# Turning the attention context on VectorE instead of TensorE, in a list-scheduled conditioned transformer block

## The chip, the cores and the metric

The kernel runs on one core of one Trainium2 chip. The metric is device time in microseconds (us), the median of several runs. Five engines work side by side and meet at semaphores: TensorE (PE; its weight loads are listed as PEld), VectorE (DVE), ScalarE (ACT), GpSimd (POOL) and SyncE (SP), which issues nearly all DMAs here. Matmul results land in PSUM, which has eight banks of 128 partitions x 512 fp32 numbers.

## The reference: what is computed

Eight sequences of 512 tokens and 256 channels go through four layers; all is fp32.

```
emb = silu(sin_emb(timestep)) @ W_ada + b_ada          # scale and shift for the norm
x   = layernorm(src) * (1 + scale) + shift
q, k, v = x @ Wq + bq, ...                             # 16 heads of 16 channels
scores = q k^T / 4 + attention_bias; masked keys = -inf
ctx = softmax(scores) @ v                              # per head, heads put side by side again
x   = x + (ctx @ Wo + bo)
x   = x + gelu2(layernorm(x) * g2 + beta2 ...) @ W2 + b2
x   = adapter(x); x = rotation(x); x = adapter(x)      # adapters of width 64, chosen by domain
```

The attention bias is 8 x 16 x 512 x 512 numbers, 134 MB, read once.

## The kernel before, in words

**Tiling.** The work of a batch is cut into 16 *units*: a head group g of four heads, and a tile qt of 128 queries. There are 128 units; n numbers them. A *half* is two query tiles; both tiles of a half in one head group are a *pair* of units. Order: batch, half, head group, tile.

**A unit** (`attention`). Four DMAs load the bias, 256 KB each, into four of 16 `bias` buffers (L898). POOL adds the mask to each (L902). PE forms four score matrices at once in four strips of its array (L910). DVE takes the bias minus the scores and its row minimum `low` (L922); ACT takes the exponential (L926), in place. Then the probabilities must be turned so that keys lie on partitions. Two ways do this. In a *turned* group, two of the four heads are transposed in 32x32 blocks by DVE (L937, `tb`) and four DMAs put the blocks in place (L946, `pT`). The other heads are transposed by PE against the identity (L961) and copied out of PSUM by ACT or DVE (`evict`, L682). `turned_groups` says which groups are turned: only group 3 in the first batch, groups 0 to 2 in the last, all in between.

**A pair.** After its second unit, PE multiplies probabilities and values (L987): `pv`, 128 x 256 in PSUM, holds four heads in four strips of 32 partitions (16 channels, then the softmax sum in row 16), with queries along the free axis. It is then brought to the layout "queries on partitions" in four steps: ACT or DVE copies pv to `pvs` (L682), PE transposes it back in two pieces (`back`, L1005), DVE takes the reciprocal of the sums (L1014) and multiplies by it (L1015) from PSUM into `ctx`.

**A half's finish** (`finish`). `half_transposed` turns ctx again by four PE transposes (L724) and copies the result out to `hT` (L682), because the output projection (L748) needs channels on partitions. Residual, layer norm, feed-forward (L1043, L1068; a gelu through ACT, POOL and DVE, L1052, L1055, L1059), two adapters with norms and the rotation, and the store (L1179) follow. The last half is finished tile by tile.

**Who sets the order.** Each step is a `Task` of a `Plan` with an engine (or a choice of ACT and DVE), a cost, what it reads and writes, and a rank. `Plan.run` plays the list through once while the kernel is built: each engine takes the ready task of the lowest rank for which buffers are free; the resulting order is then emitted as it stands, engine by engine. So costs and ranks decide the order of each engine's instructions, and who copies what out of PSUM. In that list a DMA occupies SP for its cost, and its data pass one common queue:

```
if e == DMA:
    queues = max(queues, now) + t.data
    seen = max(seen, queues)
seen += self.AFTER[e]
```

In the built program each DMA that SP issues also carries a wait for the landing of the DMA eight places before it.

The finish of half n is spread over ranks n+2 to n+11, or to n+19 for the last ones (`n < 110`). `late_weights` holds the loads of wv, bv, wo, w1, w2 (1 MB each), wd and rows2, each with a rank; `experts_matrices` fetches 16 small expert matrices by addresses that SP reads (L1210, L1214).

Of the kernel before, what the change touches and what calls it, by code (L numbers as in the profile page):

```python
# [16 lines left out]
ALU = mybir.AluOpType  # L17
AX = mybir.AxisListType

P = 128  # L20
# [49 lines left out]


class Task:
    def __init__(self, costs, emit, rank, mode, at, data):
        self.costs, self.emit, self.rank, self.data = costs, emit, rank, data
        self.engine = None
        self.mode, self.at = mode, at
        self.waits, self.then, self.buffers = 0, [], []


class Plan:  # L80

    AFTER = {PE: 0.22, DVE: 0.14, ACT: 0.16, POOL: 0.12, DMA: 2.4}

    def __init__(self):
        self.tasks, self.written, self.read = [], {}, {}
        self.rank, self.stream = 0.0, None

    def __call__(self, engine, cost, emit, r=(), w=(), mode=None, at=0.0, data=0.0):  # L90


        if isinstance(engine, dict):
            task = Task(engine, emit, self.rank, mode, at, data)
        else:
            task = Task({engine: cost}, lambda e: emit(), self.rank, mode, at, data)
        needs = []
        for key in r:
            if key in self.written:
                needs.append(self.written[key])  # L100
        for key in w:
            if key in self.written:
                needs.append(self.written[key])
            needs.extend(self.read.pop(key, ()))
        for key in r:
            self.read.setdefault(key, []).append(task)
        for key in w:
            self.written[key] = task
        for other in {id(o): o for o in needs if o is not task}.values():
            other.then.append(task)  # L110
            task.waits += 1
        for key in (*r, *w):
            buffer = key[0] if isinstance(key, tuple) else key
            if isinstance(buffer, Buffer) and buffer not in task.buffers:
                task.buffers.append(buffer)
                buffer.left += 1
        self.tasks.append(task)
        if self.stream is not None:
            self.stream.append(task)
        return task  # L120
# [23 lines left out]
    def run(self, free_at):  # L144
# [9 lines left out]
            heapq.heappush(events, (at, seq, "free", e))  # L154
            seq += 1
        idle = set()
        now, queues = 0.0, 0.0
        while events:
            now, _, what, x = heapq.heappop(events)
            if what == "ready":  # L160
# [13 lines left out]
            for e in [e for e in free_at if e in idle]:  # L174
# [29 lines left out]
                if t.mode is not None and t.mode != mode[e]:  # L204
                    cost += 1.3 if e == ACT else 0.1
                    mode[e] = t.mode
                idle.discard(e)
                t.start, t.end = now, now + cost
                order.append(t)
                heapq.heappush(events, (t.end, seq, "free", e))  # L210
                seen = t.end
                if e == DMA:
                    queues = max(queues, now) + t.data
                    seen = max(seen, queues)
                seen += self.AFTER[e]
                heapq.heappush(events, (seen, seq + 1, "over", t))
                seq += 2
# [12 lines left out]
def conditioned_sequence_kernel(  # L230
# [37 lines left out]
    SC = Slots(banks[:4])  # L268
    BG = Slots(banks[4:], SC)
    RES = slots("res", 3, [P, NT, D])  # L270
    M8 = slots("m8", 2, [P, NT, S], mybir.dt.uint8)
    NEG = slots("neg", 5, [P, S], BF16)
    MOD = slots("mod", 1, [P, 2, D])
    ROT = slots("rot", 1, [P, 2, D])
# [7 lines left out]
    PT = slots("pT", 2, [P, 4 * NT * 2 * P])  # L282
    TB = slots("tb", 2, [P, TURNED * S])
    PVS = slots("pvs", 2, [P, 2 * P])
    INV = slots("inv", 2, [P, 2, 4])
    CTX = slots("ctx", 2, [P, 2, H, HD])
    HT = slots("hT", 2, [P, NC, 2 * P])
    TMP = slots("tmp", 2, [P, 2, D])
    GT = slots("gT", 1, [P, NF, 2 * P])
# [70 lines left out]

    def turned_groups(b):

        return 3 if b == 0 else 0, NG - 1 if b == B - 1 else NG

    def rows_of(t, r, n):
        return t[:, r : r + 1, :].to_broadcast([P, n, D])
# [182 lines left out]
            b1s, cols[:, C_B1 : C_B1 + NF], AF.Copy, scale=0.851), [], ["b1s"], at=4.0)  # L549

    def late_weights():
        wo_rows = w_o.rearrange("(c m e) n -> m e c n", c=NC, e=32)

        def load(rank, cost, data, emit, key):
            plan.rank = rank
            plan(DMA, cost, emit, [], [key], data=data)

        load(-1.5, 0.45, 0.8, lambda: nc.sync.dma_start(
            wv, w_v.rearrange("(c p) n -> p c n", p=P)), "wv")
        load(-1.4, 0.4, 0.4, lambda: nc.sync.dma_start(  # L560
            bv_row, rows_in[R_BV * D : (R_BV + 1) * D].partition_broadcast(P)), "bv")
        load(2.5, 1.0, 1.0, lambda: [
            nc.sync.dma_start(wo[:, c], wo_rows[:, :HD, c]) for c in range(NC)
        ], "wo")
        load(1.1, 0.45, 3.0, lambda: nc.sync.dma_start(
            w1, w_1.rearrange("(c p) n -> p c n", p=P)), "w1")
        load(1.2, 0.45, 3.0, lambda: nc.sync.dma_start(
            w2, w_2.rearrange("(c p) n -> p c n", p=P)), "w2")
        load(2.6, 0.5, 0.5, lambda: nc.sync.dma_start(
            wd, down_w.rearrange("l (c p) a -> p l c a", p=P)), "wd")  # L570
        load(1.3, 0.4, 0.8, lambda: nc.sync.dma_start(
            rows2, rows_in[(R_GAM + 1) * D : (R_BET + 2) * D].rearrange(
                "(r d) -> r d", d=D)[::2].partition_broadcast(P)), "rows2")

    def rotations():
# [14 lines left out]
                )  # L590
            nc.sync.dma_start(cc.t[B : B + 1], rows_in[None, R_B2 * D : (R_B2 + 1) * D])

        plan(DMA, 1.0, load, [], [gb, (cc, "b2")], data=0.2)
        plan.rank = 2.5
        four = "p (g u v) -> p g u v"

# [26 lines left out]
        def store():  # L623
# [1 line left out]
            nc.sync.dma_start(turned_rows, cc.t[:B])  # L625

        plan(DMA, 0.7, store, [*((ab, u, v) for u in range(2) for v in (None, 0, 1)), (cc, "c")],
             ["rot_rows", "turned_rows"], data=0.2)

        def bias_rows():  # L630

# [7 lines left out]
            nc.sync.dma_start(wu[A1:K1, 1], turned_rows)  # L639

        plan.rank = 6.8
        plan(DMA, 1.6, bias_rows, ["turned_rows"], ["wu"], data=0.6)
        plan.rank = 7.0
        ps = Buffer(BG, lambda t: t[:, : NC * (B + 1)].rearrange("p (c b) -> p c b", c=NC))

# [112 lines left out]
    def prepare(b):  # L758
# [96 lines left out]
            for m in range(4):  # L855
                nc.sync.dma_start(to[m, :, :size], v_pad.t[32 * m : 32 * m + 32, :size])

        plan(DMA, 1.8, turned_values, [(v_pad, t) for t in range(NT)], [v_turn], data=1.0)
        negs = [Buffer(NEG) for _ in range(NT)]
        for t in range(NT):  # L860
            plan(ACT, 0.52, lambda t=t: nc.scalar.activation(
# [26 lines left out]
    def attention(u, n):  # L888
# [60 lines left out]

        if turned:  # L950
            plan(DMA, 2.5, moved, [(tb, j) for j in range(turned)], [(pT, i)],
                 data=1.05 * TURNED)
        plan.rank = n + 0.0

        whole = "p (j k i q c) -> p j k i q c"
# [22 lines left out]
        def values():  # L978
            for kc in range(NT):
# [14 lines left out]
             [(v_pad, t) for t in range(NT)] + ([v_turn] if turned else [])  # L994
             + [(pT, a, j) for a in range(2) for j in range(turned, 4)]
             + [(pT, a) for a in range(2) if turned], [pv], mode="col")
        sb = Buffer(PVS)
        evict(lambda: (
            sb.t.rearrange("p (q i c) -> p i q c", i=4, q=2),
            pv.t.rearrange("p (i q c) -> p i q c", i=4, q=2)), [pv], [sb], 0.255, 0.34)  # L1000
        pc = Buffer(BG, lambda t: t[:, : 2 * P].rearrange("p (i j e) -> p i j e", i=2, j=4))

        def back():
            for a in range(2):
                nc.tensor.transpose(  # L1005
                    pc.t[:, a].rearrange("p j e -> p (j e)"), sb.t[:, a * P : (a + 1) * P],
                    ident,
                )

        plan(PE, 0.22, back, [sb], [pc], mode="full")  # L1010
        inv = Buffer(INV)

        def normalise():
            nc.vector.reciprocal(inv.t, pc.t[:, :, :, HD])  # L1014
            nc.vector.tensor_tensor(  # L1015
                ctx_h.t[:, :, 4 * g : 4 * g + 4, :], pc.t[:, :, :, :HD],
                inv.t.unsqueeze(3).to_broadcast([P, 2, 4, HD]), ALU.mult,
            )

        plan(DVE, 0.45, normalise, [pc], [inv, (ctx_h, g)])  # L1020


    def feed_forward(res, rk, ts, store=None):
# [132 lines left out]
    def finish(b, ts, store=None):  # L1156
        res, keys = state[b][0], state[b][1]
        rk = [keys[t] for t in ts]
        rows = slice(ts[0], ts[0] + len(ts))
        ctx_h = live[(b, ts[0] // 2)]  # L1160
        cT, ck = half_transposed(
            lambda t: ctx_h.t[:, t % 2].rearrange("p h d -> p (h d)"),
            [(ctx_h, g) for g in range(NG)], ts,
        )
        token_tiles(
            len(ts),
            lambda i: [(cT.t[:, c, i * P : (i + 1) * P], wo[:, c, :]) for c in range(NC)],
            [*ck, "wo"],
            lambda ps: nc.vector.tensor_tensor(res.t[:, rows], ps, res.t[:, rows], ALU.add), rk,
        )  # L1170
        if ts[0] == 0:
            rots[b] = rot = Buffer(ROT)
            plan(DMA, 0.4, lambda: nc.sync.dma_start(
                rot.t.rearrange("p r d -> p (r d)"), rot_rows[b].partition_broadcast(P)),
                ["rot_rows"], [rot], data=0.9)
        feed_forward(res, rk, ts, store)
        adapter(b, 0, res, rk, ts)
        adapter(b, 1, res, rk, ts)
        plan(DMA, 0.42, lambda: nc.sync.dma_start(  # L1179
            out[b].rearrange("(t p) d -> p t d", p=P)[:, rows], res.t[:, rows]), rk, [],  # L1180
            data=0.4 * len(ts))
# [4 lines left out]
    def experts_matrices():  # L1186
# [19 lines left out]
        for b in range(B):  # L1206
# [10 lines left out]
                            "o p a -> (o p) a"),  # L1217
                    )

            plan(DMA, 2.0, fetch, ["expert"], [(raw, b)], data=0.2)  # L1220

        def kept():
            nc.gpsimd.tensor_tensor(
# [43 lines left out]
    for n, u in enumerate(units):  # L1267
# [5 lines left out]
        if n % 8 == 7:  # L1273
            half = n // 8 % 2
            if n + 1 < len(units):
                plan.begin()
                finish(u[0], [2 * half, 2 * half + 1])
                plan.end(n + 2.0, n + (11.0 if n < 110 else 19.0))
                continue

            for t in range(2):
                plan.begin()
                finish(u[0], [2 + t], Buffer(PT, lambda p: p.rearrange(
                    "p (c q) -> p c q", q=2 * P)[:, :NF]) if t else None)
                plan.end(n + 2.0 + 4 * t, n + 11.0 + 4 * t)
# [97 lines left out]
```

## Time and profile before

| what | value |
|---|---|
| median of 3 runs | 932.08 us (930.09 to 932.15) |
| the profiled execution's own time | 929.78 us |
| its span | 927.8 us |
| mean granted PE clock in it | 0.988 |
| DMA | 216.48 MB, 233 GB/s on average |
| bias loads / pT<-tb transfers | 512 of 256 KB / 448 of 128 KB |

How to read the profile: an engine's busy time is the time in which it has an instruction under way; matmuls overlap, so their busy times are longer than the room that they take. A group such as "L1015 DVE TENSOR_TENSOR ctx<-bank,inv" is all instructions of one line, engine and shape, as output<-inputs; after the bar stand its busy us, the mean ns of one, and the idle time of the engine just before them with what ended it. The chain of waits goes back from the last instruction, at each step to whatever released it.

### The profile page before, as it was taken

To read this page: it belongs to the slowest core of one execution; us is meant where nothing else is said; L and a number is where in the kernel's file an instruction comes from. 1 tells how busy PE (TensorE), PEld (TensorE's weight loads), DVE (VectorE), ACT (ScalarE), POOL (GpSimd) and SP (SyncE) were. 2 spreads that over 40 slices of the span, in tenths; PEclk is the share of its full clock that TensorE was granted. 3 is DMA by queue.
4 is the path that set the end of the run, shared out by engine and by line. 5 is a ranking of instruction groups with operands and counts; after the bars stand their busy time and mean duration, and the time that the engine had idled before them with its cause. 6 is when DMAs were issued, how large, how long until landed. Compare 5 with 4: busy or idle time off the path is not lost.

```text
span 927.8 us, 21009 instructions
## 1 busy us (share of the span) xinstructions
PE 893.6 (96%) x6654; PEld 591.8 (64%) x6654; DVE 788.3 (85%) x2152; ACT 752.7 (81%) x1387; POOL 754.0 (81%) x843
## 2 busy tenths in 40 slices
PE   9989999999999999999999999999999999899994
PEld 7545766566666666667666666666666676566783
DVE  4557888988988989889998889989899899999666
ACT  5957869969898889969799697987989697998553
POOL 7589899987998878978798887989789788989132
PEclk9989999999999999999999999999999999999997
DMA  9578487787977879796966979877895978978000
GB/s 318 192 240 280 151 285 230 215 285 208 300 231 233 262 235 301 203 292 216 315 216 215 303 223 281 261 247 243 251 289 164 288 229 275 288 235 270 18 24 24
DMA packets 160913, 216.48 MB, mean 233 GB/s; under 512 B 18911, under 2 KB 91657, under 8 KB 160802
## 3 DMA queue, kind: packets, MB, share of 16 engines
q1 hardware_dynamic: 160758, 215.12, 73.7%
q8 instruction: 53, 0.87, 0.4%
q14 instruction: 58, 0.48, 0.2%
q10 hardware_dynamic: 44, 0.02, 0.0%
HBM read 149.89 MB, written 4.24 MB: 166 GB/s over the span
## 4 chain that ended last, share of the span: by engine, by line
PE 59%; ACT 10%; DMA 10%; DVE 9%; POOL 6%; issue 4%; SPq 2%; POOLq 0%; DVEq 0%; ACTq 0%
PE bank L910 10%; PE bank L1068 9%; PE bank L961 9%; PE bank L1043 9%; PE bank L987 8%; PE bank L748 4%; DMA bias<-in_bias 4%; PE bank L800 4%; POOL bias L902 3%; ACT bias L926 3%; DMA pT<-tb 2%; DVE bias L922 2%; PE bank L724 2%; ACT pT L682 2%; PE bank L838 1%
## 5 line engine op out<-in xcount | busy, mean ns | idle before, releaser
L902 POOL TENSOR_TENSOR bias<-bias,neg 128x512 f32<-128x512 f32 x512 | 580.1, 1161 | 81.6 <-DMA bias<-in_bias 63.7
L926 ACT ACTIVATE bias<-bias,low 128x512 f32<-128x512 f32 x512 | 344.8, 722 | 62.0 <-DVE low L922 61.2
L922 DVE CUSTOM_DVE_ANT_0 bias<-bank,bias 128x512 f32<-128x512 f32 x512 | 329.7, 684 | 48.3 <-PE bank L910 35.2
L961 PEld LDWEIGHTS bank<-shifted,bias 128*128 128x128 f32 x1152 | 129.0, 142 | 57.1 <-issue 21.6
L961 PE MATMUL bank<-shifted,bias 128*128 128x128 f32 x1152 | 159.3, 279 | 4.5 <-ACT pT L682 2.3
L937 DVE STREAM_TRANSPOSE tb<-bias 128x512 f32<-128x512 f32 x224 | 148.0, 691 | 11.1 <-DMA pT<-tb 8.6
L910 PE MATMUL bank<-kT,qz 32*128 32x512 f32 x1024 | 155.2, 645 | 2.0 <-DVE low L922 1.9
L682 ACT COPY pT<-bank 128x512 f32<-128x512 f32 x209 | 114.3, 588 | 36.1 <-PE bank L961 34.5
L1043 PE MATMUL bank<-hT,w 128*128 128x256 f32 (+1 forms) x544 | 127.1, 374 | 2.1 <-ACT pT L682 0.8
L987 PE MATMUL bank<-pT,v_pad 128*32 128x256 f32 x1152 | 123.0, 382 | 0.0
L1068 PE MATMUL bank<-w,gT 128*128 128x256 f32 x496 | 117.8, 384 | 0.1
L987 PE MATMUL bank<-pT,v_turn 128*32 128x256 f32 x896 | 107.6, 382 | 2.0 <-DMA pT<-tb 2.0
L1043 PEld LDWEIGHTS bank<-hT,w 128*128 128x128 f32 x544 | 94.2, 190 | 23.9 <-issue 4.0
L1068 PEld LDWEIGHTS bank<-w,gT 128*128 128x128 f32 x496 | 90.4, 190 | 26.8 <-issue 13.5
L987 PEld LDWEIGHTS bank<-pT,v_turn 128*32 128x32 f32 x896 | 48.0, 109 | 49.7 <-issue 5.3
L910 PEld LDWEIGHTS bank<-kT,qz 32*128 32x128 f32 x1024 | 44.0, 184 | 46.6 <-issue 26.8
L1055 POOL TENSOR_SCALAR sig<-sig 128x512 f32<-128x512 f32 (+1 forms) x68 | 40.5, 596 | 40.1 <-ACT sig L1052 35.0
L1052 ACT ACTIVATE sig<-bank,b1s 128x256 f32<-128x256 f32 (+1 forms) x136 | 55.0, 456 | 9.9 <-PE bank L1043 9.4
L1059 DVE SCALAR_TENSOR_TENSOR gT<-bank,cols,sig 128x256 f32<-128x256 f32 (+1 forms) x128 | 53.5, 464 | 10.5 <-POOL sig L1055 10.4
L987 PEld LDWEIGHTS bank<-pT,v_pad 128*32 128x32 f32 x1152 | 54.8, 109 | 7.9 <-issue 1.9
L690 DVE BATCH_NORM_STATS2 st<-res 128x6 f32<-128x256 f32 x128 | 52.3, 409 | 5.4 <-DMA res<-in_x 3.5
L682 DVE COPY pT<-bank 128x512 f32<-128x512 f32 x79 | 52.5, 682 | 3.8 <-PE bank L961 3.4
(142 smaller groups left out, 1156.3 us busy)
## 6 DMA issues: line engine op xcount, KB each, us to landing
bias<-in_bias SPq DMA_DIRECT2D x512, 256.0 KB
pT<-tb SPq DMA_DIRECT2D x448, 128.0 KB
out<-res SPq DMA_DIRECT2D x15, 256.0 KB
res<-in_x SPq DMA_DIRECT2D x7, 512.0 KB
v_turn<-v_pad SPq DMA_DIRECT2D x32, 68.0 KB
m<-in_mask SPq DMA_DIRECT2D x8, 256.0 KB
w<-in_w SPq DMA_DIRECT2D x2, 1024.0 KB
mod<-ada_rows SPq DMA_DIRECT2D x8, 256.0 KB
```

The lines of the kernel that those rows point to most:

```text
L682: nc.scalar.copy(*pair()) if e == ACT else nc.vector.tensor_copy(*pair())), r, w)
L902: plan(POOL, 1.12, lambda j=j: nc.gpsimd.tensor_tensor(dif[j].t, dif[j].t, negs[qt].t, ALU.add), [negs[qt]], [dif[j]])
L910: nc.tensor.matmul(sc[j].t, qz.t[strip, par, c, qs], kT.t[strip, c, :], start=True, stop=True,)
L922: plan(DVE, 0.61, lambda j=j: nc.vector.tensor_tensor_reduce(dif[j].t, sc[j].t, dif[j].t, -1.0, 3.0e38, ALU.add, ALU.min, low.t[:, j : j + ...
L926: plan(ACT, 0.61, lambda j=j: nc.scalar.activation(dif[j].t, dif[j].t, AF.Exp, bias=low.t[:, j : j + 1], scale=-1.0), [(low, j)], [dif[j]] ...
L937: plan(DVE, 0.62, lambda j=j: nc.vector.transpose(tb.t.rearrange("p (m h k c) -> h p k m c", m=4, h=TURNED, k=NT)[j], dif[j].t.rearrange(" ...
L961: nc.tensor.transpose(ps.t[:, kc, :], dif[j].t[:, kc * P : (kc + 1) * P], ident)
L987: nc.tensor.matmul(pv.t[32 * j : 32 * j + 32, :], (v_turn if j < turned else v_pad).t[:, at : at + 32], pj, start=(kc == 0), stop=(kc == N ...
L1043: nc.tensor.matmul(ps.t[:, i, :w], w1[:, c, f * P : (f + 1) * P], hT.t[:, c, :w], start=(c == 0), stop=(c == NC - 1),)
L1052: plan(ACT, 0.155 + 0.1 * n, lambda i=i, f=f, ps=ps, sg=sg: nc.scalar.activation(sg.t[:, i, :w], ps.t[:, i, :w], AF.Tanh, bias=b1s[:, f : ...
L1059: plan(DVE, 0.14 + 0.13 * n, lambda i=i, f=f, ps=ps, sg=sg: nc.vector.scalar_tensor_tensor(gT.t[:, f, :w], ps.t[:, i, :w], cols[:, C_B1 + ...
L1068: nc.tensor.matmul(ps.t[:, i, :], gT.t[:, f, i * P : (i + 1) * P], w2[:, f, :], start=(f == 0), stop=(f == NF - 1),)
```

## The change

The context no longer passes PE on its way from the values to the output projection. DVE transposes pv in 32x32 blocks straight out of PSUM into `pvs`, so that queries lie on partitions within each block; reciprocal and multiplication work on that in SBUF and write `zed`, which holds two head groups side by side (32 channels per block); every second head group, DVE transposes zed in blocks into `ctx`, now laid out with channels on partitions. Within a strip of 32 partitions the channels stand in another order than before, so the rows of wo are loaded to match, by eight DMAs instead of two. `finish` uses ctx as it is.

The list changes too: a DMA task may consist of `many` transfers, each of which starts only when the one eight places before it has landed, and the common queue starts with a backlog of 9 us. Ranks of the weight loads change (wo 2.5 to 3.0, w1 1.1 to 3.1, w2 1.2 to 4.1). There is one mask buffer instead of two. In the last batch all four groups are turned. The longer spread of the finish starts at n = 100 instead of 110.

```diff
+    BACKLOG = 9.0
+    FLIGHT = 8
...
+                if e == DMA:
+                    begun = now
+                    for _ in range(t.many):
+                        begun = max(begun, landed[-self.FLIGHT]) + cost / t.many
+                        queues = max(queues, begun) + t.data / t.many
+                        landed.append(queues + 1.5)
+                    cost = begun - now
...
                 if e == DMA:
-                    queues = max(queues, now) + t.data
-                    seen = max(seen, queues)
+                    seen = max(seen, queues - 0.4)
...
-    M8 = slots("m8", 2, [P, NT, S], mybir.dt.uint8)
+    M8 = slots("m8", 1, [P, NT, S], mybir.dt.uint8)
...
-        return 3 if b == 0 else 0, NG - 1 if b == B - 1 else NG
+        return (NG - 1 if b == 0 else 0), NG
...
-        load(2.5, 1.0, 1.0, lambda: [
-            nc.sync.dma_start(wo[:, c], wo_rows[:, :HD, c]) for c in range(NC)
-        ], "wo")
-        load(1.1, 0.45, 3.0, lambda: nc.sync.dma_start(
+        load(3.0, 3.6, 1.0, lambda: [
+            nc.sync.dma_start(wo[32 * j : 32 * j + 32, c], wo_rows[c, j, :, :HD])
+            for c in range(NC) for j in range(4)
+        ], "wo", many=8)
+        load(3.1, 0.45, 3.0, lambda: nc.sync.dma_start(
             w1, w_1.rearrange("(c p) n -> p c n", p=P)), "w1")
-        load(1.2, 0.45, 3.0, lambda: nc.sync.dma_start(
+        load(4.1, 0.45, 3.0, lambda: nc.sync.dma_start(
             w2, w_2.rearrange("(c p) n -> p c n", p=P)), "w2")
...
-        sb = Buffer(PVS)
-        evict(lambda: (
-            sb.t.rearrange("p (q i c) -> p i q c", i=4, q=2),
-            pv.t.rearrange("p (i q c) -> p i q c", i=4, q=2)), [pv], [sb], 0.255, 0.34)
-        pc = Buffer(BG, lambda t: t[:, : 2 * P].rearrange("p (i j e) -> p i j e", i=2, j=4))
-
-        def back():
-            for a in range(2):
-                nc.tensor.transpose(
-                    pc.t[:, a].rearrange("p j e -> p (j e)"), sb.t[:, a * P : (a + 1) * P],
-                    ident,
-                )
-
-        plan(PE, 0.22, back, [sb], [pc], mode="full")
-        inv = Buffer(INV)
+        sb, inv = Buffer(PVS), Buffer(INV)
+        plan(DVE, 0.37, lambda: nc.vector.transpose(
+            sb.t.rearrange("p (i b c) -> p b i c", i=2, c=32),
+            pv.t.rearrange("p (b i c) -> p b i c", i=2, c=32)), [pv], [sb])
+        if par == 0:
+            live[(b, half, c)] = Buffer(ZED)
+        zed = live[(b, half, c)]
 
         def normalise():
-            nc.vector.reciprocal(inv.t, pc.t[:, :, :, HD])
+            of = sb.t.rearrange("p (b e) -> p b e", e=32)
+            nc.vector.reciprocal(inv.t, of[:, :, HD])
             nc.vector.tensor_tensor(
-                ctx_h.t[:, :, 4 * g : 4 * g + 4, :], pc.t[:, :, :, :HD],
-                inv.t.unsqueeze(3).to_broadcast([P, 2, 4, HD]), ALU.mult,
+                zed.t[:, :, par, :], of[:, :, :HD],
+                inv.t.unsqueeze(2).to_broadcast([P, 8, HD]), ALU.mult,
             )
 
-        plan(DVE, 0.45, normalise, [pc], [inv, (ctx_h, g)])
+        plan(DVE, 0.45, normalise, [sb], [inv, (zed, par)])
+        if par == 1:
+            plan(DVE, 0.35, lambda: nc.vector.transpose(
+                ctx_h.t[:, c, :], zed.t.rearrange("p b u d -> p (b u d)")),
+                [(zed, 0), (zed, 1)], [(ctx_h, c)])
...
-        cT, ck = half_transposed(
-            lambda t: ctx_h.t[:, t % 2].rearrange("p h d -> p (h d)"),
-            [(ctx_h, g) for g in range(NG)], ts,
-        )
         token_tiles(
             len(ts),
-            lambda i: [(cT.t[:, c, i * P : (i + 1) * P], wo[:, c, :]) for c in range(NC)],
-            [*ck, "wo"],
+            lambda i: [
+                (ctx_h.t[:, c, (ts[i] % 2) * P : (ts[i] % 2 + 1) * P], wo[:, c, :])
+                for c in range(NC)
+            ],
+            [(ctx_h, c) for c in range(NC)] + ["wo"],
...
-                plan.end(n + 2.0, n + (11.0 if n < 110 else 19.0))
+                plan.end(n + 2.0, n + (11.0 if n < 100 else 19.0))
```

More of the change, by code (lines that the diff above doesn't have):

```diff
@@ L72, with __init__ @@
 class Task:
-    def __init__(self, costs, emit, rank, mode, at, data):
+    def __init__(self, costs, emit, rank, mode, at, data, many):
         self.costs, self.emit, self.rank, self.data = costs, emit, rank, data
         self.engine = None
-        self.mode, self.at = mode, at
+        self.mode, self.at, self.many = mode, at, many
         self.waits, self.then, self.buffers = 0, [], []
@@ L88, in __init__, with __call__ @@
         self.rank, self.stream = 0.0, None
-    def __call__(self, engine, cost, emit, r=(), w=(), mode=None, at=0.0, data=0.0):
+    def __call__(self, engine, cost, emit, r=(), w=(), mode=None, at=0.0, data=0.0, many=1):
         if isinstance(engine, dict):
-            task = Task(engine, emit, self.rank, mode, at, data)
+            task = Task(engine, emit, self.rank, mode, at, data, many)
         else:
-            task = Task({engine: cost}, lambda e: emit(), self.rank, mode, at, data)
+            task = Task({engine: cost}, lambda e: emit(), self.rank, mode, at, data, many)
         needs = []
@@ L156, in run @@
         idle = set()
-        now, queues = 0.0, 0.0
+        now, queues = 0.0, self.BACKLOG
+        landed = [self.BACKLOG + 1.5] * self.FLIGHT
         while events:
@@ L284, in conditioned_sequence_kernel @@
     PVS = slots("pvs", 2, [P, 2 * P])
-    INV = slots("inv", 2, [P, 2, 4])
-    CTX = slots("ctx", 2, [P, 2, H, HD])
+    INV = slots("inv", 2, [P, 8])
+    ZED = slots("zed", 2, [P, 8, 2, HD])
+    CTX = slots("ctx", 2, [P, NC, 2 * P])
     HT = slots("hT", 2, [P, NC, 2 * P])
@@ L551, in late_weights, with load @@
     def late_weights():
-        wo_rows = w_o.rearrange("(c m e) n -> m e c n", c=NC, e=32)
-        def load(rank, cost, data, emit, key):
+        wo_rows = w_o.rearrange("(c u j e) n -> c j u e n", c=NC, u=2, e=32)
+        def load(rank, cost, data, emit, key, many=1):
             plan.rank = rank
-            plan(DMA, cost, emit, [], [key], data=data)
+            plan(DMA, cost, emit, [], [key], data=data, many=many)
         load(-1.5, 0.45, 0.8, lambda: nc.sync.dma_start(
@@ L591, in load @@
             nc.sync.dma_start(cc.t[B : B + 1], rows_in[None, R_B2 * D : (R_B2 + 1) * D])
-        plan(DMA, 1.0, load, [], [gb, (cc, "b2")], data=0.2)
+        plan(DMA, 1.0, load, [], [gb, (cc, "b2")], data=0.2, many=3)
         plan.rank = 2.5
@@ L627, in rotations @@
         plan(DMA, 0.7, store, [*((ab, u, v) for u in range(2) for v in (None, 0, 1)), (cc, "c")],
-             ["rot_rows", "turned_rows"], data=0.2)
+             ["rot_rows", "turned_rows"], data=0.2, many=2)
         def bias_rows():
@@ L641, in rotations @@
         plan.rank = 6.8
-        plan(DMA, 1.6, bias_rows, ["turned_rows"], ["wu"], data=0.6)
+        plan(DMA, 1.6, bias_rows, ["turned_rows"], ["wu"], data=0.6, many=4)
         plan.rank = 7.0
@@ L856, in turned_values @@
                 nc.sync.dma_start(to[m, :, :size], v_pad.t[32 * m : 32 * m + 32, :size])
-        plan(DMA, 1.8, turned_values, [(v_pad, t) for t in range(NT)], [v_turn], data=1.0)
+        plan(DMA, 1.8, turned_values, [(v_pad, t) for t in range(NT)], [v_turn], data=1.0, many=4)
         negs = [Buffer(NEG) for _ in range(NT)]
@@ L951, in attention @@
             plan(DMA, 2.5, moved, [(tb, j) for j in range(turned)], [(pT, i)],
-                 data=1.05 * TURNED)
+                 data=1.05 * TURNED, many=4)
         plan.rank = n + 0.0
@@ L1218, in fetch @@
                     )
-            plan(DMA, 2.0, fetch, ["expert"], [(raw, b)], data=0.2)
+            plan(DMA, 2.0, fetch, ["expert"], [(raw, b)], data=0.2, many=2)
         def kept():
```

## The prediction

> **What bounds the kernel now.** I read the page first: busy time by engine.
>
> ```profile
> PE 893.6 (96%) x6654; PEld 591.8 (64%) x6654; DVE 788.3 (85%) x2152; ACT 752.7 (81%) x1387; POOL 754.0 (81%) x843
> ```
>
> TensorE (PE) is busy almost throughout. That is an average, so next come the stages: busy us and instructions per engine, granted clock, DMA share, GB/s.
>
> ```profile
> 39.00:77.00 38.00, 32.89 (x214) 17.08 (x217) 20.51 (x58) 23.82 (x48) 29.23 (x27) 0.87 0.71 228
> 77.00:851.00 774.00, 758.18 (x5772) 497.61 (x5771) 694.36 (x1879) 660.99 (x1194) 670.58 (x714) 1.00 0.80 251
> 851.00:889.00 38.00, 38.00 (x296) 28.76 (x293) 26.71 (x70) 22.85 (x47) 13.11 (x20) 1.00 0.18 54
> 889.00:928.00 39.00, 26.97 (x164) 21.11 (x163) 24.92 (x72) 16.25 (x46) 11.57 (x30) 0.85 0.06 21
> ```
>
> Three stages: a ragged start to 77 us, a long steady part (77 to 851) with PE 98% busy and VectorE (DVE) second at 694.36/774 = 90%, and a tail. In the tail PE has no gap until about 907 us; the last 20 us are one tile's serial chain. So work taken from PE shortens the steady part, as long as DVE does not take over.
>
> **What leaves PE.** "Busy" overstates a matmul, because matmuls overlap; its share of the path is read from the chain of waits (start, us, what).
>
> ```profile
> 859.54 0.22 PE bank L1005 x2
> ...
> 863.15 1.75 PE bank L961 x16
> ...
> 880.20 0.44 PE bank L724 x4
> ```
>
> A pair of turn-backs (L1005) costs 0.22 us here and 0.37 us in three of the seven places it has on the chain after 780 us; the mean is 0.28. So 64 pairs x 0.28 = 18.2 us. The context's turn before the output projection (L724): 16 halves x 0.44 = 7.0. In the last batch one more head group takes the VectorE-and-DMA route: 4 units x 2 heads x 4 transposes (L961) x 0.109 (1.75/16) = 3.5. Scores, values and projections keep their counts. PE loses 28.7 us.
>
> **What DVE and ACT gain and lose.** Groups of instructions: count, busy us, mean ns.
>
> ```profile
> L937 DVE STREAM_TRANSPOSE tb<-bias 128x512 f32<-128x512 f32 x224 | 148.0, 691 | 11.1 <-DMA pT<-tb 8.6 <-ACT bias L926 1.9 <-ACT sig L1052 0.3
> L682 DVE COPY pT<-bank 128x512 f32<-128x512 f32 x79 | 52.5, 682 | 3.8 <-PE bank L961 3.4
> L1015 DVE TENSOR_TENSOR ctx<-bank,inv 128x128 f32<-128x128 f32 x64 | 18.7, 292 | 2.2
> L682 DVE COPY hT<-bank 128x512 f32<-128x512 f32 x27 | 18.3, 679 | 3.4 <-PE bank L724 3.2
> L682 ACT COPY pvs<-bank 128x256 f32<-128x256 f32 x46 | 16.8, 366 | 11.2 <-PE bank L987 11.2
> L682 DVE COPY pvs<-bank 128x256 f32<-128x256 f32 x18 | 7.3, 408 | 4.4 <-PE bank L987 4.4
> ```
>
> New on DVE: 64 block transpositions of 128x256 out of PSUM. No row shows one. Below stands the copy of the same tile out of the same bank, 0.408; above, the transposition of twice as many elements, 0.691. Copies of 256 and 512 elements stand as 408 to 679, so 0.6 x 0.691 = 0.42, near the lower end; 64 x 0.42 = 26.9 us. Then 32 transpositions from SBUF (same bounds, same value): 13.4. The extra head group: 8 x 0.691 = 5.5. Reciprocal and multiplication keep their counts; their source moves from PSUM to SBUF. The nearest pair of rows is DVE's 128x256 addition, 434 ns with both inputs in SBUF (L1149) and 404 with one in PSUM (L1169): between -2 and +2 us in 64, taken as nothing.
>
> Gone from DVE: 18 copies of pvs, 7.3. The list also shares the remaining copies out afresh; in the program as built DVE has 18 fewer hT copies (18 x 0.679 = 12.2) and 20 fewer pT copies (20 x 0.664, its busy mean, = 13.3). DVE's sum: 26.9 + 13.4 + 5.5 - 7.3 - 12.2 - 13.3 = +13.0 us. ACT loses 46 x 0.366 = 16.8 and takes 12 pT and 3 hT copies (8.3): -8.5. POOL's work is unchanged.
>
> A rule against the change: the Trainium skill, "SBUF — State Buffer", section "Who interferes with whom", says that a VectorE instruction with two SBUF inputs contends with a GpSimd instruction that reads SBUF. L1015 has one input in PSUM today and takes 292 ns; its successor has both in SBUF. By that page, with POOL busy 87% of the steady part in pieces of 1.16 us, an estimate is 64 x 0.87 x 0.58 = 32 us more on DVE, and the whole would come to about 922 us. No row here shows it: the two L1149 on DVE ran at 911 to 917 us, when POOL hardly worked.
>
> **The steady part.** Some 56 of the 64 pairs, 14 of the 16 halves and half of the extra head group lie in 77 to 851: 15.7 + 6.2 + 1.7 = 23.6 us less PE work. PE alone would give 774 - 23.6 = 750. DVE: 694.4 + 11.4 = 705.8 busy; its idle time there is 79.6. If none of that goes, the stretch is 785. By the table of waits about 74 of DVE's 139.5 idle us end with a PE instruction (53%), the first of them
>
> ```profile
> DVE bias L922 <- PE bank L910: 35.2, 46, 5.1
> ```
>
> and those shrink when PE is earlier: without them 705.8 + 37.4 = 743. Between 743 and 785 I take two thirds of PE's 23.6: **-16 us**. What is late next is DVE, at 705.8/758 = 93%, then POOL at 88%; the DMA engines go from 0.80 to 0.82, with 16 more pT transfers (2.1 MB) at the end of it.
>
> **The start.** In 39 to 77 us PE ran 214 instructions; at the steady rate (1,752 in 77 to 309 us) it would be 287. The missing 73 are 9.7 us. The cause, in the timelines of SP and POOL (start, us, what; in brackets the idle time before it):
>
> ```profile
> 33.33 8.03 SPq L1214 DMA_DIRECT2D gT<-in_experts  x8
> 41.49 1.93 SPq L898 DMA_DIRECT2D bias<-in_bias  x4
> ```
>
> ```profile
> 44.85 4.49 POOL L902 TENSOR_TENSOR bias<-bias,neg 128x512 f32<-128x512 f32 x4 [10.14 <-DMA bias<-in_bias]
> ```
>
> POOL stands still for 10 us because unit 4's bias loads are issued behind both 1 MB weights and eight expert loads. In the changed program these four come before wd, wo and all expert loads; w1 follows unit 5's loads and w2 unit 6's. Against it: wo is loaded by eight DMAs instead of two, at 0.61 us of SP each (v_turn's four took 2.45): 4.9 - 1.4 = 3.5 us of SP, in front of unit 5's loads; unit 4's also stand behind mod, which waits for ada_rows to land; and every DMA there waits for the eighth one before it. With one mask buffer the second mask waits for ScalarE's four L861, done at 12.8 us, before SP gets there: nothing. Bounds 0 and -10; unit 4 was the whole stall, so nearer the far one: **-7 us**.
>
> **The tail.** PE loses 5 pairs x 0.22, two halves x 0.44 and two units' turned heads (1.75): 3.7 us, passed on while PE has no gap. The very last units now wait for a DMA (pieces pT<-tb on the chain are 2 to 6 us); after the last values at 874.5 PE had 33 us of other work, which hides this. Without that cover: +4. Moving the finish of half 103 later (100 for 110) only shifts PE work into that cover. Between -4 and +4: **-2 us**.
>
> **Sum.** 929.8 (the profiled execution's own time; span 927.8) - 16 - 7 - 2 = 904.8. The median of the three runs is 2.3 above that execution; I add half: **906 us**.
>
> **Rivals.**
> - *All of it arrives*: PE keeps the pace and the start closes: 929.8 - 28.7 - 10 = 891. For it: PE's 98%. Against: DVE would have to run at 94%.
> - *DVE takes over*: its idle shrinks only so far that the steady part stays at 774; start and tail remain: 921. The same region is reached if the start gains nothing (913).
> - *Slower*: DVE becomes the bound in the steady part. Its idle time stays at 79.6 because it comes from in-order waits on POOL, ACT and DMA, and the PSUM transposition costs 0.55: 705.8 + 7.3 + 79.6 = 793, +19; with -9 elsewhere 940. It decides from 783 us on: at 0.42 each if 77 of the 79.6 idle us stay, at 0.69 if 62 do. Against: over half of that idle is PE's own lateness.
> - *The change does not do what it says* (the list's knowledge of eight DMAs moves nothing that is late): this costs the start's 7 alone, 913.
>
> **How the numbers follow.** Forecast (898 to 912) 0.45; all of it (886 to 898) 0.17; DVE takes over or no gain at the start (912 to 927) 0.20; no change 0.07; slower 0.11. A difference under 0.3% (2.8 us) can't be told from none. The range 889 to 927 leaves out the best part of the second case and the last two. Faster 0.82, same 0.07, slower 0.11.
>
> **What would show it.** Right: matmuls 224 fewer; PE still 96% or more in the steady part, DVE at 93%, the new transpositions at 0.40 to 0.45 us; POOL's 10 us gap near 35 to 45 us gone and that stage at the granted clock 1.00. Wrong: PE well under 95% in the steady part with DVE at 95%; the multiplication well over 0.3 us; a new gap at unit 5 behind wo's loads; PE idle at the last values.

## The result and the profile after

The changed kernel takes 930.44 us (median of 19 runs, 925.21 to 937.89); the kernel before, on the same chips, 931.02 us (19 runs). The ratio is 0.9999, with a 95% interval of 0.9983 to 1.0016: no change, where 906 us was forecast. The profiled execution has a span of 926.3 us.

The page's line of busy times, then the stages of the changed kernel (columns as before: stage, its length, busy us and instructions of PE, PEld, DVE, ACT and POOL, granted clock, DMA share, GB/s):

```profile
PE 887.0 (96%) x6430; PEld 576.8 (62%) x6430; DVE 827.4 (89%) x2197; ACT 748.6 (81%) x1357; POOL 755.3 (82%) x843
```

```profile
39.00:77.00 38.00, 33.55 (x258) 19.82 (x257) 31.79 (x71) 29.10 (x56) 27.05 (x28) 0.96 0.69 221
77.00:851.00 774.00, 753.29 (x5522) 482.90 (x5521) 719.01 (x1904) 650.74 (x1153) 668.91 (x708) 0.99 0.81 253
851.00:889.00 38.00, 37.64 (x285) 26.92 (x284) 31.29 (x81) 24.75 (x50) 15.48 (x23) 1.00 0.38 106
889.00:928.00 39.00, 24.96 (x154) 19.49 (x153) 23.76 (x70) 15.67 (x45) 11.47 (x30) 0.86 0.06 21
```

PE has 224 matmuls fewer, as counted, but DVE has 39.1 us more busy time instead of 13.0. In the long stage DVE is at 719.01/774 = 93%, and PE got through 5,522 matmuls in the 774 us where it had 5,772 before; so the 97% busy no longer means as much work done. In the chain of waits that ended last, as shares of the span, DVE's part has more than doubled. The kernel before, then the changed one:

```profile
PE 59%; ACT 10%; DMA 10%; DVE 9%; POOL 6%; issue 4%; SPq 2%; POOLq 0%; DVEq 0%; ACTq 0%
```

```profile
PE 51%; DVE 21%; ACT 12%; DMA 6%; issue 4%; POOL 3%; SPq 1%; DVEq 0%; POOLq 0%; ACTq 0%
```

The groups of instructions show which new DVE work is dear (count, busy us, mean ns, idle before):

```profile
L1011 DVE STREAM_TRANSPOSE pvs<-bank 128x256 f32<-128x256 f32 x64 | 27.8, 435 | 10.9 <-PE bank L998 9.1 <-ACT kT L833 1.4
L1021 DVE TENSOR_TENSOR zed<-pvs,inv 128x128 f32<-128x128 f32 x64 | 49.0, 766 | 2.2
L1028 DVE STREAM_TRANSPOSE ctx<-zed 128x256 f32<-128x256 f32 x32 | 14.2, 444 | 1.0
```

The transpositions cost what was expected. The multiplication (L1021) does not: it was 292 ns with its large input in PSUM, and is 766 ns now that both inputs lie in SBUF. The worst single one is in the start. First DVE, then POOL in the changed kernel's timeline (start, us, what):

```profile
45.80 0.20 DVE L1020 RECIPROCAL inv<-pvs 128x8 f32<-128x8 f32 x1
46.04 5.88 DVE L1021 TENSOR_TENSOR zed<-pvs,inv 128x128 f32<-128x128 f32 x1
51.84 1.28 DVE L693 COPY pT<-bank 128x512 f32<-128x512 f32 x2
```

```profile
45.37 0.71 POOL L629 TENSOR_TENSOR hT<-hT,pvs 8x256 f32<-8x256 f32 x1 [1.14 <-ACT pvs L619]
46.05 4.49 POOL L913 TENSOR_TENSOR bias<-bias,neg 128x512 f32<-128x512 f32 x4
50.52 1.25 POOL L888 TENSOR_TENSOR res<-res,mod 128x512 f32<-128x512 f32 x1
```

POOL ran five instructions without a gap, and the multiplication ended 0.15 us after the last of them (51.77). PE then had a gap of 4.44 us that a copy by DVE ended. Over all 64 multiplications of this execution: 15 took 0.29 to 0.33 us; the other 49 all began while a POOL instruction ran, and all ended 0.15 to 0.16 us after the end of one. The excess over 0.291 us adds up to 30.4 us, 5.6 of it from that single one.

Two ordinary cases, each POOL first, then DVE. In the first, the multiplication waits for the first of two additions and gets in before the second is done:

```profile
180.40 2.32 POOL L913 TENSOR_TENSOR bias<-bias,neg 128x512 f32<-128x512 f32 x2 [0.80 <-DVE low L933]
```

```profile
180.92 0.78 DVE L1021 TENSOR_TENSOR zed<-pvs,inv 128x128 f32<-128x128 f32 x1
```

In the second, POOL's instruction has two elements per partition, and the multiplication doesn't wait:

```profile
756.67 0.70 POOL L709 TENSOR_TENSOR rstd<-rstd,neg_half 128x2 f32<-128x2 f32 x1
```

```profile
756.97 0.29 DVE L1021 TENSOR_TENSOR zed<-pvs,inv 128x128 f32<-128x128 f32 x1
```

### The profile page after: what moved, and what is told of

It reads as the page before. It is cut to its first block, busy times and chain, and to the rows that moved or that the text cites. A ratio compares the mean times of both kernels' runs of the same rounds, so it can differ in the third digit from the quotient of the medians.

```text
span 926.3 us, 20595 instructions
## 1 busy us (share of the span) xinstructions
PE 887.0 (96%) x6430; PEld 576.8 (62%) x6430; DVE 827.4 (89%) x2197; ACT 748.6 (81%) x1357; POOL 755.3 (82%) x843
## 4 chain that ended last, share of the span: by engine, by line
PE 51%; DVE 21%; ACT 12%; DMA 6%; issue 4%; POOL 3%; SPq 1%; DVEq 0%; POOLq 0%; ACTq 0%
PE bank L921 9%; PE bank L972 8%; PE bank L998 8%; PE bank L1078 7%; DVE bias L933 7%; PE bank L1053 6%; PE bank L811 5%; ACT bias L937 4%; DVE tb L948 3%; DMA pT<-tb 3%; DMA bias<-in_bias 3%; PE bank L759 2%; DVE st L701 2%; ACT sig L1062 1%; PE bank L410 1%
## 5 line engine op out<-in xcount | busy, mean ns | idle before, releaser
L913 POOL TENSOR_TENSOR bias<-bias,neg 128x512 f32<-128x512 f32 x512 | 582.0, 1164 | 84.8 <-DMA bias<-in_bias 57.1
L933 DVE CUSTOM_DVE_ANT_0 bias<-bank,bias 128x512 f32<-128x512 f32 x512 | 326.1, 679 | 21.2 <-PE bank L921 20.9
L972 PEld LDWEIGHTS bank<-shifted,bias 128*128 128x128 f32 x1120 | 126.1, 142 | 78.7 <-ACT bias L937 33.7
L972 PE MATMUL bank<-shifted,bias 128*128 128x128 f32 x1120 | 157.9, 280 | 12.7 <-DVE pT L693 5.1
L921 PE MATMUL bank<-kT,qz 32*128 32x512 f32 x1024 | 166.4, 642 | 1.5 <-DVE low L933 1.3
L948 DVE STREAM_TRANSPOSE tb<-bias 128x512 f32<-128x512 f32 x232 | 153.6, 689 | 10.8 <-DMA pT<-tb 6.3
L693 ACT COPY pT<-bank 128x512 f32<-128x512 f32 x221 | 121.4, 584 | 40.5 <-PE bank L972 39.6
L998 PE MATMUL bank<-pT,v_turn 128*32 128x256 f32 x928 | 112.7, 385 | 2.8 <-DMA pT<-tb 1.6
L1053 PEld LDWEIGHTS bank<-hT,w 128*128 128x128 f32 x544 | 93.8, 190 | 30.4 <-issue 12.2
L921 PEld LDWEIGHTS bank<-kT,qz 32*128 32x128 f32 x1024 | 50.9, 183 | 54.2 <-issue 26.6
L998 PEld LDWEIGHTS bank<-pT,v_turn 128*32 128x32 f32 x928 | 50.2, 110 | 52.5 <-issue 9.8
L1021 DVE TENSOR_TENSOR zed<-pvs,inv 128x128 f32<-128x128 f32 x64 | 49.0, 766 | 2.2
```

Of the source, the lines that this page charges most:

```text
L693: nc.scalar.copy(*pair()) if e == ACT else nc.vector.tensor_copy(*pair())), r, w)
L913: plan(POOL, 1.12, lambda j=j: nc.gpsimd.tensor_tensor(dif[j].t, dif[j].t, negs[qt].t, ALU.add), [negs[qt]], [dif[j]])
L921: nc.tensor.matmul(sc[j].t, qz.t[strip, par, c, qs], kT.t[strip, c, :], start=True, stop=True,)
L933: plan(DVE, 0.61, lambda j=j: nc.vector.tensor_tensor_reduce(dif[j].t, sc[j].t, dif[j].t, -1.0, 3.0e38, ALU.add, ALU.min, low.t[:, j : j + ...
L948: plan(DVE, 0.62, lambda j=j: nc.vector.transpose(tb.t.rearrange("p (m h k c) -> h p k m c", m=4, h=TURNED, k=NT)[j], dif[j].t.rearrange(" ...
L972: nc.tensor.transpose(ps.t[:, kc, :], dif[j].t[:, kc * P : (kc + 1) * P], ident)
```

## The experiments

Each is compared with the kernel before on the same chip. The runs were spread over four chips, so where two runs of different chips are set against each other, the ratios are what counts. Three theories were put up after the result: (1) the multiplication with two SBUF inputs waits for GpSimd, and that takes what PE gives; (2) the list's new order loses what the context gains; (3) the engines are so full and so tied by in-order waits that a saving no longer shows.

### The reciprocals in PSUM, and the two parts of the change alone

Run `e1_inv_psum`, on the changed kernel:

```diff
...
-            nc.vector.reciprocal(inv.t, of[:, :, HD])
+            inv = pv.home.tiles[pv.slot][:, 2 * P : 2 * P + 8]
+            nc.vector.reciprocal(inv, of[:, :, HD])
...
-        plan(DVE, 0.45, normalise, [sb], [inv, (zed, par)])
+        plan(DVE, 0.45, normalise, [sb], [pv, (zed, par)])
```

> The changed kernel with one edit: the eight reciprocals per query are written into unused columns of the PSUM bank that still holds the values, so the multiplication has one input in SBUF and one in PSUM. Theory 1 (the port that VectorE shares with GpSimd): the multiplication falls from 0.77 to about 0.29 us, VectorE loses about 30 us of busy time, and the whole goes to 903 to 914 us. Theory 2 (the list's new order costs what the context gains): 0.29 too, but the time stays at 925 to 931. Theory 3 (all engines are so nearly full and so tied by in-order waits that work taken from one of them no longer shows): 0.29, VectorE 30 us less busy, time 922 to 931.

Run `e2_context_alone`: the changed kernel with the `Plan.run` of before, ranks 2.5, 1.1 and 1.2 for wo, w1 and w2, `turned_groups` of before, and `n < 110`.

> The context part of the change with the list as it was before (no limit of eight, old ranks of the weight loads, last batch with three turned groups, old spread of the finish); the one mask buffer stays, for room. Theory 1: still about 930, because the slow multiplication is still there; it shows 0.7 to 0.8 us. Theory 2: 905 to 915, since the list does the harm. Theory 3: 925 to 932.

Run `e3_list_alone`: the converse, the context code and wo's two DMAs of before in the changed kernel's list.

> The kernel before with the list's part of the change alone (limit of eight, backlog, ranks of the weight loads, one mask buffer, four turned groups in the last batch, longer spread of the finish); the context goes by TensorE as before. Theory 1: 920 to 930, a little faster from the start. Theory 2: 940 to 955. Theory 3: 925 to 932.

Run `e4_context_alone_inv_psum`: both edits, of e1 and of e2.

> Second and first together: the context part alone, old list, with the reciprocals in PSUM. Theory 1: 908 to 920 (the gain of the steady part without that of the start). Theory 2: 905 to 915, no better than the context part alone. Theory 3: 922 to 931.

| kernel | median us | ratio to before | 95% interval | multiplication, mean ns |
|---|---|---|---|---|
| changed | 930.44 | 0.9999 | 0.9983 to 1.0016 | 766 |
| e1, reciprocals in PSUM | 908.79 | 0.9753 | 0.9727 to 0.9779 | 287 |
| e2, context alone | 950.73 | 1.0210 | 1.0181 to 1.0239 | 649 |
| e3, list alone | 921.51 | 0.9895 | 0.9869 to 0.9920 | 292 |
| e4, context alone, reciprocals in PSUM | 926.45 | 0.9940 | 0.9910 to 0.9970 | 287 |

One edit brings the changed kernel to 908.79 us. Theory 2 is refuted: the list alone is faster than before. Theory 3 is refuted for the changed kernel's list, since e1 lies well below its 922 to 931: DVE is 33.7 us less busy there, and it shows. With the new list, the changed kernel's zero is made of two effects: the list makes 10 us (e3), and the context as written loses them again.

With the old list the forecasts of theory 1 were missed. The context as written loses 19 us there (e2), outside what any theory had written down. Moving eight numbers per partition, which here too makes the list hold the bank longer, gains 24 us (e2 to e4), but e4 at 926.45 lies above theory 1's 908 to 920 and inside theory 3's range: the context without the collision gains only 5 us with the old list and 12.7 with the new one (e3 to e1). So the two parts of the change do not simply add up; why is not shown.

The groups of e1, to be read against those of the changed kernel above:

```profile
L1011 DVE STREAM_TRANSPOSE pvs<-bank 128x256 f32<-128x256 f32 x64 | 28.0, 437 | 13.4 <-PE bank L998 11.5 <-ACT bias L937 1.8
L1022 DVE TENSOR_TENSOR zed<-pvs,bank 128x128 f32<-128x128 f32 x64 | 18.4, 287 | 2.2
L1029 DVE STREAM_TRANSPOSE ctx<-zed 128x256 f32<-128x256 f32 x32 | 14.2, 445 | 1.1
```

and two of its stages:

```profile
39.00:77.00 38.00, 37.20 (x299) 21.92 (x296) 29.22 (x78) 31.04 (x58) 27.18 (x28) 1.00 0.68 212
77.00:851.00 774.00, 745.69 (x5621) 484.86 (x5619) 706.31 (x1935) 667.80 (x1191) 676.93 (x718) 1.00 0.82 256
```

In the same 774 us PE does 99 matmuls more than in the changed kernel, with DVE less busy.

### A control for the order, and the price per instruction

Holding the bank longer changes what the list does, so e1 is two changes. Run `e5_bank_held` has the same program as e1, instruction for instruction on every engine, but for the place of the reciprocals:

```diff
-        plan(DVE, 0.45, normalise, [sb], [inv, (zed, par)])
+        plan(DVE, 0.45, normalise, [sb], [inv, pv, (zed, par)])
```

> A control for the run with the reciprocals in PSUM, which also held the bank of the values longer and so got another order from the list. Here the list holds the bank just as long, every engine has the very same instructions in the same order, and only the place of the eight reciprocals differs: SBUF again. Theory 1 (two SBUF inputs wait for GpSimd): the multiplication takes 0.6 to 0.8 us again and the whole 925 to 936. Rival (the other order made the gain): 905 to 915.

Measured: 923.12 us, ratio 0.9923 (0.9897 to 0.9950). The line of its multiplication (duration ns min/median/max):

```profile
L1021 DVE TENSOR_TENSOR zed<-pvs,inv x64: 291/677/5856, 45.8 to 872.6; 128x128 f32<-128x128 f32 x64
```

So of e1's gain about 16 us (ratios 0.9923 to 0.9753; 14 by the medians of the two chips) belong to the place of the reciprocals and about 7 (0.9999 to 0.9923) to the order that came with holding the bank. Neither answer that was written down covers 923: it lies between.

Run `e6_tiny_two_sbuf`, on e1, adds after each multiplication

```diff
+            nc.vector.tensor_tensor(
+                INV.tiles[n // 2 % 2], sb.t[:, 0:8], sb.t[:, 8:16], ALU.add
+            )
```

> The version with the reciprocals in PSUM, and after each multiplication one more VectorE addition of 8 elements with both inputs in SBUF, whose result nobody reads (64 in all; order otherwise the same). If an instruction with two SBUF inputs must wait until GpSimd's running instruction ends, whatever its size: 0.5 to 0.8 us each in the mean, ending shortly after the end of a GpSimd instruction, and 920 to 935 in all. If contention is a matter of elements moved: about 0.2 us each and 909 to 914 in all.

Measured: 926.08 us, ratio 0.9957 (0.9929 to 0.9986), 0.0204 over e1's ratio, some 19 us. The added instruction, 8 elements per partition:

```profile
L1026 DVE TENSOR_TENSOR inv<-pvs x64: 157/560/5521, 45.7 to 874.7; 128x8 f32<-128x8 f32 x64
```

It can be done in 0.157 us, has a median of 0.56 and once takes 5.5. Of the 64, 54 ended 0.01 to 0.06 us after the end of a POOL instruction. The wait is for the instruction that POOL runs, not for elements moved: eight numbers wait as long as 128. In all, its 64 cost DVE 42 us, 32 of them waiting.

### Two other ways out

Run `e7_pool_multiplies` leaves the reciprocals on DVE (cost 0.2) and gives the multiplication to GpSimd:

```diff
...
+        plan(POOL, 0.4, lambda: nc.gpsimd.tensor_tensor(
+            zed.t[:, :, par, :], sb.t.rearrange("p (b e) -> p b e", e=32)[:, :, :HD],
+            inv.t.unsqueeze(2).to_broadcast([P, 8, HD]), ALU.mult,
+        ), [sb, inv], [(zed, par)])
```

> The changed kernel with the multiplication given to GpSimd, which then can't collide with itself; VectorE keeps the reciprocals and transpositions. Theory 1: VectorE about 49 us less busy than in the changed kernel, GpSimd 22 to 30 us more, whole 900 to 918. Rival (GpSimd, 82% busy, becomes the bound, or its long queue delays the context): 920 to 935.

Measured: 910.81 us, ratio 0.9791 (0.9760 to 0.9822). The rival falls: POOL takes 0.403 us for each and goes to 775.6 us busy, which it can bear; DVE falls from 827.4 to 783.6. The list's order is another one here too, so the 20 us are not the collision's alone.

```profile
L1023 POOL TENSOR_TENSOR zed<-pvs,inv 128x128 f32<-128x128 f32 x64 | 25.8, 403 | 6.7 <-DVE inv L1018 6.5
```

Run `e8_list_knows` only tells the list the true price:

```diff
-        plan(DVE, 0.45, normalise, [sb], [inv, (zed, par)])
+        plan(DVE, 0.92, normalise, [sb], [inv, (zed, par)])
```

> The changed kernel with one number: the list is told that reciprocal and multiplication take 0.92 us together instead of 0.45, so it gives VectorE fewer copies. Theory 1: the waiting itself remains, so most of the loss remains: 920 to 929. Rival (the order was merely wrong about the cost): 905 to 914.

Measured: 930.28 us, ratio 1.0003 (0.9970 to 1.0037). Nothing comes of it, a little less than theory 1's 920 to 929: DVE gets 12 pT copies fewer (47 instead of 59), but its multiplications wait longer (854 ns in the mean), and it is still 826.8 us busy. The true price in the list does not remove the wait.

### What the list's 10 us consist of

From e3, with only some of its three pieces: the knowledge of eight DMAs with the backlog ("flight"), the later ranks of wo, w1 and w2 ("ranks"), and the fourth turned group with `n < 100` ("tail"). First "flight" alone (`e9_flight_alone`):

> Of the list's part alone (context by TensorE) only the knowledge of eight DMAs under way and the backlog; ranks, turned groups and the spread of the finish as before; one mask buffer. In its program unit 4's bias loads again stand ahead of the expert loads, but behind w1 and w2. If this knowledge is what the start gains by: 920 to 925, GpSimd's gap of 10 us gone. If the weights' ranks are: 928 to 933.

"Ranks" alone (`e10_ranks_alone`):

> Only the later ranks of wo, w1 and w2. In its program unit 4's bias loads still stand behind three expert fetches and w1 and w2. If the knowledge of eight is what matters: 929 to 934 with a gap of some 10 us on GpSimd before 50 us. If the ranks are: 920 to 925.

"Tail" alone (`e11_tail_alone`):

> Only the fourth turned group of the last batch and the longer spread of the finish from unit 100. The prediction gave the tail 2 us: 927 to 931. Rival (the waits for the last blocks' DMAs reach the end): 932 to 936.

"Flight" and "ranks" (`e13_flight_and_ranks`):

> Context by TensorE, the knowledge of eight DMAs and the later ranks of the weights together, the tail as before. If these two need each other (the first brings unit 4's loads forward, the second takes 2 MB of weights out of their way): 921 to 926. If the gain of the list needs the tail's part: 929 to 933.

"Flight" and "tail" (`e14_flight_and_tail`):

> The same with the tail's part in place of the ranks. If the ranks are needed: 928 to 932. If the tail is what keeps the start's lead: 920 to 926.

| kernel | median us | ratio to before | 95% interval |
|---|---|---|---|
| e9, flight | 930.72 | 0.9979 | 0.9962 to 0.9997 |
| e10, ranks | 932.12 | 0.9999 | 0.9983 to 1.0016 |
| e11, tail | 931.62 | 0.9991 | 0.9973 to 1.0009 |
| e13, flight and ranks | 926.93 | 0.9971 | 0.9958 to 0.9985 |
| e14, flight and tail | 923.84 | 0.9943 | 0.9925 to 0.9961 |
| e3, all three | 921.51 | 0.9895 | 0.9869 to 0.9920 |

No piece makes 10 us alone, and the 920 to 925 forecast for flight (e9) was missed although POOL's gap there shrinks from 10.1 to 3.6 us. With flight, the tail seems to add more than the ranks (e14, e13), but their intervals overlap. Ranks and tail without flight were not run, so it is not shown that the others need flight. In the traces flight does what was hoped for at the start: unit 8's scores begin at 67.6 us instead of 76.9. But the lead goes again: at unit 32 both are at 233 us. The stages show where. The kernel before, then e9:

```profile
77.00:90.00 13.00, 12.83 (x111) 7.25 (x111) 10.80 (x35) 11.06 (x20) 11.53 (x12) 1.00 0.93 316
90.00:300.00 210.00, 207.37 (x1564) 137.44 (x1562) 187.21 (x504) 176.12 (x320) 186.82 (x198) 1.00 0.76 236
```

```profile
39.00:77.00 38.00, 37.67 (x279) 21.29 (x278) 25.17 (x71) 30.93 (x59) 25.65 (x27) 1.00 0.57 168
77.00:90.00 13.00, 9.34 (x86) 5.70 (x83) 7.64 (x20) 5.24 (x9) 11.07 (x10) 0.87 0.91 287
90.00:300.00 210.00, 203.52 (x1522) 132.61 (x1521) 185.07 (x504) 175.68 (x318) 189.11 (x199) 1.00 0.79 248
```

The start runs 279 matmuls instead of 214; the next 13 us run 86 instead of 111, on a DMA share of 0.91 and a granted PE clock of 0.87, and the 210 us after them 42 fewer. 65 matmuls won, 67 given back. The DMA share was no lower in the kernel before (0.93); why the lead goes is not shown.

Run `e12_inv_psum_old_tail` asks for the tail where DVE is not stalled: e1 with three turned groups in the last batch and `n < 110`.

> The version with the reciprocals in PSUM, but three turned groups in the last batch and the spread of the finish as before. If the new tail gains 2 us: 909 to 913. Rival (it costs, now that TensorE is the less full of the two): 902 to 907.

Measured: 913.26 us, ratio 0.9785 (0.9758 to 0.9813). Against e1's 0.9753 (0.9727 to 0.9779) the new tail looks worth some 3 us, but the intervals overlap; the time lies just above the first forecast, and the rival's falls.

## Why the prediction was wrong, point by point

- **What bounds the kernel**: right. PE paced the long stage with DVE next, and when DVE got too much its part of the chain of waits went from 9% to 21%. PE at 97% and DVE at 93% in the long stage are what the prediction named as signs of being right; they came without the gain.
- **What leaves PE**: the count of 224 is right; that PE's time was worth having is borne out by e1 (908.79 against e3's 921.51).
- **The new transpositions**, 0.42 us each with bounds 0.408 and 0.691: 0.435 and 0.444. Right.
- **Reciprocal and multiplication "taken as nothing"**: this is the step that failed. Between -2 and +2 us was allowed; the multiplications took 30 us more (18.7 to 49.0), because 49 of 64 waited for a POOL instruction. Of the 24 us by which the time was missed this explains about 16 (e5 to e1); another 7 hang on the order that holding the bank brings (changed kernel to e5). The row chosen as nearest, DVE's addition with two SBUF inputs (L1149, 434 ns), ran when POOL hardly worked, and the text said so in the next paragraph but kept its zero. In the kernel before, every other DVE instruction with two tensor inputs in the tables takes one of them from PSUM, so no row could show the price. Moving a source from PSUM to SBUF was priced by the memory's speed; what it cost was the other engine's time.
- **The rule of the Trainium skill** ("SBUF — State Buffer", section "Who interferes with whom": a VectorE instruction with two SBUF inputs contends with a GpSimd instruction that reads SBUF) was weighed and set aside because no row showed it. Its estimate, 32 us of DVE, is close to what the runs show, 30.4, in part by luck: 49 instructions waited, not 56, and one of them alone made 5.6 us; in e2 the excess is 22.9. What the prediction made of it, 922 us, was too early a time; the measured is 930.
- **The steady part, -16**: with the collision gone, the context's share is 921.51 (e3) to 908.79 (e1), -12.7 with the new list, for the whole kernel and with the order that holding the bank brings; with the old list it is only -5 (e4). So the size was nearly right at best, for a kernel that was not this one. In the changed kernel units 16 to 104 take 603.3 us against 595.9 before.
- **The start, -7**: POOL's 10 us gap is gone and unit 8 begins 5 us earlier. But of the cause only half was right. The two 1 MB weights were the lesser part: with them still ahead (e9) the gap of 10.1 us falls to 3.6, and with only the weights late (e10) to 6.8. The stage ran at a granted clock of 0.96, not 1.00, with PE's 4.44 us gap after the long multiplication in it. And the gain was not carried on to the end, which the sum had taken for granted: of the 5 us 1.1 are left at unit 16, and in e1, without the collision, 1.9 of 8.3.
- **The tail, -2**: not contradicted; with the list's knowledge of DMAs it makes some 7 us by the ratios (0.9971 in e13, 0.9895 in e3), alone nothing clear of noise (e11). In the changed kernel the stretch from unit 104 to the end takes 198.5 us against 206.3, which pays for the loss in the units before.
- **Sum**: 906 was missed by 24; e1, one edit away, is at 908.79. The slower rival named DVE as the bound and DMA, POOL and ACT as reasons, but priced the wrong new instruction.

What stays open: why the order that comes with holding the bank is 7 us better (changed kernel to e5), with the same 30 us of waiting; why the list and the context make more together than apart; and why the list's three pieces together make more than their sum.

## What to carry to other kernels

When an edit turns a VectorE instruction's PSUM operand into a second SBUF operand, ask what GpSimd is doing at that time: the price is not the instruction's length but mostly the rest of the instruction that GpSimd is running, once per instruction, however small. If GpSimd is busy most of the time with large tiles in SBUF, keep one operand in PSUM (even a tiny one will do) or give the operation to GpSimd. And a lead won at the start is only worth what is left of it some units later: follow the same unit through both traces before it goes into a sum.

## What the runs showed of the hardware that was not expected

- A VectorE instruction with two SBUF inputs that began beside a large GpSimd instruction waited for that one's end and then got in, even where GpSimd's next followed without a gap. So it was in 39 of the 49 that waited; 46 of the 49 waited for one GpSimd instruction alone. GpSimd pays little: the 36 bias additions that came next took 1.20 to 1.24 us, while none of the 512 before took over 1.19; over all 512 the mean goes from 1,161 to 1,164 ns.
- The multiplication at 46 us is the exception: it let five GpSimd instructions go by, 5.88 us for 0.29 us of work. In e5 and e6 an instruction waited as long at the same place (5.86 and 5.52 us). Why there is open.
- Not every GpSimd instruction holds it up. Beside the one of two elements per partition (`rstd`, L709) the multiplication took 0.29 us with 0.40 us of that instruction still to come, and 0.31 us in e5 with 0.69 us to come.
- The side of the operand decides, not its size. In e1 the large input comes from SBUF and eight numbers per partition from PSUM: 286 to 290 ns for all 64, not one of them delayed, though 58 began while a GpSimd instruction ran.
- GpSimd took 403 ns for the multiplication that VectorE does in 291 undisturbed and in 766 in the mean beside GpSimd's work; here the engine that is slower by itself is the better place.
